# A message-passing kernel on one core: operands in PSUM, loads in turn, stores placed anew

## The chip, the cores and the metric

The kernel runs on one core of a Trainium2 chip. The metric is the device time of one execution in microseconds (us), as the median of several runs. The engines are PE (matrix products; PEld is its weight load), DVE (VectorE), ACT (ScalarE), POOL (GpSimd) and SP (SyncE, which here only issues transfers). Each works through its own queue of instructions in order, and semaphores tie them together. SBUF is the on-chip memory that all of them read; PSUM is the small memory into which PE writes its products, in banks[...].

## What is computed

A graph has 12,500 nodes with 96 features and 412,500 edges, which are sorted by their target node. Three small layers, each with a batch norm over all its rows, give node features, edge features and messages; the messages are summed per target.

```python
def _mlp(h, W, b, gamma, beta):
    h = relu(h @ W + b)
    mu, var = mean(h, axis=0), mean(square(h - mu), axis=0)
    return gamma * (h - mu) * rsqrt(var + EPS) + beta

node_feat = _mlp(x, W_node, ...)
edge_feat = _mlp(edge_attr, W_edge, ...)
row, col = edge_index
message = concatenate([x[row], x[col], edge_feat], axis=1)
message = _mlp(message, W_msg, ...)
agg = segment_sum(message, col)
out = layernorm(x + agg + node_feat)
```

## The kernel before

**Tables.** x[row] @ W_msg's first third is the same for all edges of a source node, so the kernel makes a table of it for all nodes, p_tab in DRAM, and for the targets q_tab. `table()` (L144 to L160) makes either in 7 stretches of 14 blocks: products of x (`xp`, in SBUF) with the weights (L154), copies to `trow` by DVE and ACT (L156, L158), a store (L159), then a `yield`, at which the caller puts other work in between. The loads of x in 7 chunks (L96 to L98) alternate between SP's and ACT's queues, all ahead of everything else, and the source numbers `src` follow on ACT (L99).

**Gathers.** Edges are worked on in tiles of 128, groups of 4 tiles and blocks of 4 groups: 202 blocks. A tile's 128 rows of p_tab are fetched by one indirect transfer that POOL issues (L166), 16 for a block. The first 26 blocks are gathered early, while the other stages run: `blocks()` (L171 to L178) gathers a block into one of two tiles `stage`, and SP stores it to `spill` in DRAM (L177), from where the main loop reads it back as `pb`. Each `next(store)` sets one such step in SP's and POOL's order. The first 3 blocks gather rows of x, not of p_tab, and are converted later. The other 176 blocks are gathered into a ring of 25 group tiles `pg`, the first 25 of them after the last early block (L357), each other one when an older tile has been used.

**Stages.** First p_tab, 0 to about 84 us. Then small loads (L190 to L201), and `rel` (L203 to L223), each edge's target less the first target of its block: a subtraction on DVE (L209) of `basei` from `dsti`, where `basei` is the row `base` broadcast to 128 partitions by a transfer (L207). Then q_tab, `places()` (L225 to L243), which subtracts `first` from the targets in another layout (L239) and stores them, `nodes()` (L245 to L275: the node layer, its norm, and x + node_feat sent to DRAM as `y0_d`), and `edge_norm()` (L277 to L329), which runs the edge layer over all edges for its mean and variance: products L294 into PSUM, ReLU by ACT L298, statistics by DVE L300. It loads its input and yields every 8 blocks. In these stages SP and POOL keep the order in which the program lists their work (`manual_schedule`). The places of `next(store)`: after stretches 2 and 5 of p_tab; 0, 2 and 5 of q_tab, and once after it; after steps 0, 4 and 10 of `nodes()`; and in `edge_norm()` spread over its yields by `73 * i >= 50 + 100 * n`.

**Main loop** (L502 to L534), about 1030 to 5250 us. A step k is a group; all engines keep the listed order. In step k: `linear(k+1)` (L447 to L453, PE: z from edge features and target rows, 4 tiles of 96 columns), `message(k)` (L455 to L473, DVE and ACT), `sums(k-2)` (L484, PE: sums per target in a window of 31 nodes, and the Gram matrix for the norm), once per block `edges` (L437, PE) and `prepare` (L444 ACT, L445 DVE) for the next block and `add` (L497, L498, DVE) for an older one; then POOL's gathers for a tile further ahead. In `message`, at the first group of a block (i == 0), DVE writes into h for the whole block which of 31 nodes each edge belongs to (L461: `rel` is compared with `iota`, 4 x 31 node numbers in SBUF). Then hs = z + pg (L467) for the group, which frees its ring tile, and after every second group ACT's ReLU (L469). I call the four sums of a block hs0 to hs3, and block s's first z z(4s). Per block DVE's order is L461, hs0, hs1, hs2, L445, L497 twice, L498, hs3. z has two PSUM tiles, used in turn.

After the loop a last stage (L705 on) applies the message norm and the layer norm per node.

Of the kernel before, what the change touches and what calls it, by code (L numbers as in the profile page):

```python
# [11 lines left out]
F32 = mybir.dt.float32  # L12
I32 = mybir.dt.int32
AF = mybir.ActivationFunctionType
OP = mybir.AluOpType
# [61 lines left out]
def gnn(ctx, tc, t):  # L77
# [15 lines left out]
    ring = rpool.enter_context(tc.tile_pool(name="ring", bufs=RING))  # L93
    xp = xpool.enter_context(tc.tile_pool(name="x", bufs=1)).tile([C, XW], F32, name="xp")
    nc.scalar.dma_start(w_msg, t["L0_gnn_W_msg"].rearrange("(s k) f -> k s f", k=C))
    for i in range(0, NB, CH):  # L96
        part = slice(COL[i], COL[i + CH] if i + CH < NB else XW)
        (nc.scalar if i // CH % 2 else nc.sync).dma_start(xp[:, part], t["xp"][:, part])  # L98
    nc.scalar.dma_start(src, t["src"])  # L99

    ident = const.tile([P, P], F32, name="ident")
    make_identity(nc, ident)
# [18 lines left out]
    agg = const.tile([C + 1, WT], F32, name="agg")  # L121
    rel = const.tile([P, NGP, GT], F32, name="rel")
    base = const.tile([1, NBL], I32, name="base")
    mstat = const.tile([C, 2], F32, name="mstat")
    vec = const.tile([C, len(_VECS)], F32, name="vec")
    v = {name[7:]: vec[:, i:i + 1] for i, name in enumerate(_VECS)}
# [17 lines left out]
    def table(out, w, work, ps, queues, bufs):  # L144

        rows = out.rearrange("(p b) f -> p b f", b=NB)
        for c in range(0, NB, CH):
            r = work.tile([P, CH, C], F32, name="trow", bufs=3)
            for j, i in enumerate(range(0, CH, NBK)):
                n = min(NBK, CH - i)  # L150
                pt = ps.tile([P, NBK, C], F32, name="pt", bufs=bufs)
                for g in range(n):
                    k = COL[c + i + g]
                    nc.tensor.matmul(pt[:, g, :], xp[:, k:k + P], w, start=True, stop=True)  # L154
                if j % 2:
                    nc.scalar.activation(r[:, i:i + n, :], pt[:, :n, :], AF.Copy)  # L156
                else:
                    nc.vector.tensor_copy(r[:, i:i + n, :], pt[:, :n, :])  # L158
            queues[c // CH % len(queues)].dma_start(rows[:, c:c + CH, :], r)  # L159
            yield  # L160
# [18 lines left out]


    store = blocks()
    with tc.manual_schedule(engines={ET.SP, ET.Pool}):
        with tc.tile_pool(name="win_w", bufs=1) as work, tc.tile_pool(name="win_ps", bufs=2, space=PSUM) as ps:
            for i, _ in enumerate(table(p_tab, w_msg[:, 0, :], work, ps, (nc.sync, nc.scalar), 4)):
                if i in (2, 5):
                    next(store)

# [2 lines left out]
    nc.sync.dma_start(vec, t["vecs"])  # L190
    nc.sync.dma_start(w_node, t["L0_gnn_W_node"])
    nc.sync.dma_start(b_msg, t["L0_gnn_b_msg"])
    nc.sync.dma_start(base, t["base"])
    for i in range(NS):
        k, n = Q * i, C - Q * i
        nc.sync.dma_start(wide[k:k + EK, :n], t["wb"][:, C - n:])
# [6 lines left out]
    with tc.tile_pool(name="win", bufs=1) as win, tc.tile_pool(name="win_ps", bufs=2, space=PSUM) as ps:  # L203
        dsti = win.tile([P, NGP, GT], I32, name="dsti")
        nc.sync.dma_start(dsti, t["dst"].rearrange("p (g t) -> p g t", t=GT))
        basei = win.tile([P, NBL], I32, name="basei")
        nc.sync.dma_start(basei, t["base"].to_broadcast([P, NBL]))  # L207
        by_block = "p (b g) t -> p b (g t)"
        nc.vector.tensor_tensor(rel.rearrange(by_block, g=BG), dsti.rearrange(by_block, g=BG),  # L209
                                basei.unsqueeze(2).to_broadcast([P, NBL, BG * GT]), op=OP.subtract)  # L210
        worst = win.tile([P, 2, BG], F32, name="worst")
        for k in range(BG):
            nc.vector.tensor_reduce(worst[:, 0, k:k + 1], rel[:, k:NG:BG, :], axis=AX.XY, op=OP.max)
            nc.vector.tensor_reduce(worst[:, 1, k:k + 1], rel[:, k:NG:BG, :], axis=AX.XY, op=OP.min)
        out = win.tile([P, 1], F32, name="out")
        nc.vector.tensor_sub(worst[:, 0, :], worst[:, 0, :], iota[:, :, WN - 1])
        nc.vector.tensor_sub(worst[:, 1, :], iota[:, :, 0], worst[:, 1, :])
        nc.vector.tensor_reduce(out, worst.rearrange("p a k -> p (a k)"), axis=AX.X, op=OP.max)
        po = ps.tile([1, P], F32, name="po", bufs=1)
        nc.tensor.transpose(po, out, ident)  # L220
        most = win.tile([1, 1], F32, name="most")
        nc.vector.tensor_reduce(most, po, axis=AX.X, op=OP.max)
        nc.vector.tensor_scalar(flag, most, 0.0, None, op0=OP.is_gt)  # L223

    def places():  # L225

        with tc.tile_pool(name="lin", bufs=2) as work, tc.tile_pool(name="lin1", bufs=1) as one:
            first = one.tile([P, RW], I32, name="first")
            nc.sync.dma_start(first, t["first"])
            rows = rel_d.rearrange("o (p g e) -> (o p) g e", g=RW, e=GE)  # L230
            parts = [slice(i, min(i + 2, RW)) for i in range(0, RW, 2)]
            lins = []
            for i in range(len(parts) + 1):
                if i < len(parts):
                    n = parts[i].stop - parts[i].start
                    lins.append(work.tile([P, n, GE], I32, name="lin"))
                    nc.sync.dma_start(lins[i], t["dlin"][:, parts[i], :])
                    rlin = work.tile([P, n, GE], F32, name="rlin")
                    nc.vector.tensor_tensor(rlin, lins[i], first[:, parts[i]].unsqueeze(2).to_broadcast([P, n, GE]),  # L239
                                            op=OP.subtract)  # L240
                    lins[i] = rlin
                if i:
                    nc.sync.dma_start(rows[:, parts[i - 1], :], lins[i - 1])  # L243
# [87 lines left out]
    def fast(ring):  # L331
# [3 lines left out]
        with tc.manual_schedule(engines={ET.SP, ET.Pool}):  # L335
            with tc.tile_pool(name="tab_w", bufs=1) as work, tc.tile_pool(name="tab_ps", bufs=2, space=PSUM) as ps:
                for i, _ in enumerate(table(q_tab[WM:WM + NN, :], w_msg[:, 1, :], work, ps, (nc.sync,), 8)):
                    if i in (0, 2, 5):
                        next(store)
            next(store)  # L340
            nc.sync.dma_start(q_tab[:WM, :], zero[:WM])
            for r in range(WM + NN, WT, 64):
                n = min(64, WT - r)
                nc.sync.dma_start(q_tab[r:r + n, :], zero[:n])
            places()
            for i, _ in enumerate(nodes()):
                if i in (0, 4, 10):
                    next(store)
            xpool.close()
            n = 0  # L350
            for i, _ in enumerate(edge_norm()):
                if 73 * i >= 50 + 100 * n:
                    next(store, None)
                    n += 1
            for _ in store:
                pass
            got = {g: ahead_of(g) for g in range(SPILL, SPILL + RING)}  # L357
# [11 lines left out]
        with tc.tile_pool(name="fix", bufs=1) as fix, tc.tile_pool(name="msg", bufs=2) as work, \  # L369
# [11 lines left out]
            hb = [fix.tile([P, BG, GT, P], F32, name=f"h{i}") for i in range(HB)]  # L381
            for x in hb:
                nc.vector.memset(x[:, :, :, C:C + 1], 1.0)

            eas, block, prs, zs, pas, pair = {}, {}, {}, {}, {}, [None]

# [60 lines left out]
            def linear(k):  # L447
                s, g = steps[k]
                n = min(GT, NT - g * GT)
                zs[k] = ps.tile([P, GT, C], F32, name="z")  # L450
                for i in range(n):
                    nc.tensor.matmul(zs[k][:, i, :], left[s % 2][:KR, g % BG, i * P:(i + 1) * P],  # L452
                                     rhs[:KR, s % RB, g % BG, :], start=True, stop=True)  # L453

            def message(k):  # L455
                s, g = steps[k]
                n = min(GT, NT - g * GT)
                i = g % BG
                h, z, pg = hb[s % HB], zs.pop(k), got.pop(g)
                if i == 0:  # L460
                    nc.vector.tensor_tensor(  # L461
                        h[:, :, :, C + 1:C + 1 + WN], rel[:, g:g + BG, :].unsqueeze(3).to_broadcast([P, BG, GT, WN]),
                        iota.unsqueeze(2).to_broadcast([P, BG, GT, WN]), op=OP.is_equal)
                if i % 2 == 0:
                    pair[0] = work.tile([P, 2, GT, C], F32, name="hs")
                hs = pair[0]
                nc.vector.tensor_add(hs[:, i % 2, :n, :], z[:, :n, :], pg[:, :n, :])  # L467
                if i % 2 and n == GT:
                    nc.scalar.activation(h[:, i - 1:i + 1, :, :C], hs, AF.Relu)  # L469
                elif i % 2 or g == NG - 1:  # L470
                    for o in range(i // 2 * 2, i + 1):
                        m = GT if o < i else n
                        nc.scalar.activation(h[:, o, :m, :C], hs[:, o % 2, :m, :], AF.Relu)  # L473
# [301 lines left out]
```

## Time and profile before

| what | value |
|---|---|
| median of 3 runs | 5365.1 us (5362.86 to 5375.22) |
| profiled execution | 5383.58 us; its span, first to last instruction, 5381.9 us |
| granted clock of PE, mean | 0.662 |
| 0 to 284 us: tables, rel, places, nodes | POOL busy 157.4 us, PE 156.7, DVE 118.1 |
| 284 to 980 us: edge_norm | PE busy 401.4 us, DVE 359.3, POOL 336.8, ACT 293.0 |
| 1030 to 5250 us: main loop | PE busy 2717.8 us, POOL 2594.5, PEld 2133.8, DVE 1153.4, ACT 697.9 |
| 5250 to 5382 us: last groups, last stage | PE busy 108.3 us, DVE 78.3 |

The slices of the span, each a fortieth (134.5 us):

```profile
PE   5557653566666666666666666666666666765668
DVE  1446542622222222223222223222232223222225
POOL 5553455255566666666666665666666666666660
PEclk9755555566766666666676676666666666667667
```

A digit is the busy share in tenths; the last row is the clock that PE was granted, in tenths of full speed. Slices 1 and 2 are the tables and nodes, 3 to 7 edge_norm, 8 to 39 the main loop, 40 the end. A row of a group of instructions, as the profile has it, gives line, engine, operation, output<-inputs with shapes and count, then the busy time in all and the mean of one in ns, then the idle time of the engine just before them and what ended most of it. A timeline row gives the start, the duration, the engine and line, and in brackets the idle time before it and what ended it.

### The profile page before, as it was taken

What the parts mean: (1) busy time and instruction counts of PE and PEld (TensorE: products, weight loads), DVE (VectorE), ACT (ScalarE), POOL (GpSimd) and SP (SyncE); (2) the same over time, 40 slices, a digit from 0 to 9 for tenths busy, and PEclk for the clock granted to TensorE, in tenths of its full rate; (3) what the DMA queues carried; (4) which work ended last, traced back from release to release, by engine and by line L of the source; (5) the groups of instructions that cost most, each with busy time, mean ns of one, the idle gap of its engine ahead of it and who ended that gap; (6) DMA issues with size and microseconds to landing.
All of it is one profiled execution on the core that took longest, in us unless ns stands there. A gap on an engine that the chain in (4) does not pass through costs nothing. (4 is left out here: it accounts for less than half of the span.)

```text
span 5381.9 us, 46696 instructions
## 1 busy us (share of the span) xinstructions
PE 3389.5 (63%) x16705; PEld 2576.6 (48%) x16705; DVE 1708.3 (32%) x2635; ACT 1077.3 (20%) x1015; POOL 3088.7 (57%) x3231
## 2 busy tenths in 40 slices
PE   5557653566666666666666666666666666765668
PEld 5423321354545555445554445454555544554557
DVE  1446542622222222223222223222232223222225
ACT  0235432311111111111111111111111111111112
POOL 5553455255566666666666665666666666666660
PEclk9755555566766666666676676666666666667667
DMA  5333322111111111111111111111111111111112
GB/s 165 127 87 66 71 62 50 27 37 33 39 44 37 43 43 43 44 37 43 43 43 41 45 36 43 43 42 44 37 43 42 42 45 36 43 43 42 45 36 83
DMA packets 154401, 270.78 MB, mean 50 GB/s; under 512 B 83463, under 2 KB 83976, under 8 KB 153154
## 3 DMA queue, kind: packets, MB, share of 16 engines
q0 software_dynamic: 103136, 158.62, 13.8%
q1 hardware_dynamic: 47936, 98.39, 6.4%
q10 hardware_dynamic: 3088, 10.71, 0.6%
q8 instruction: 133, 2.18, 0.2%
q14 instruction: 108, 0.88, 0.1%
HBM read 225.88 MB, written 41.60 MB: 50 GB/s over the span
## 5 line engine op out<-in xcount | busy, mean ns | idle before, releaser
L166 POOL DMA_INDIRECT pg<-p_tab,src x2807 | 2689.2, 958 | 1785.6 <-DVE hs L467 953.3
L452 PE MATMUL z<-rhs,left 128*128 128x96 f32 x6446 | 1221.4, 337 | 886.4 <-issue 766.5
L452 PEld LDWEIGHTS z<-rhs,left 128*128 128x128 f32 x6446 | 1094.8, 248 | 1181.1 <-issue 987.6
L484 PE MATMUL pa<-h 128*97 128x128 f32 x6446 | 1241.8, 331 | 522.8 <-issue 519.7
L484 PEld LDWEIGHTS pa<-h 128*97 128x97 f32 x6446 | 1012.0, 209 | 628.3 <-issue 626.2
L467 DVE TENSOR_TENSOR hs<-z,pg 128x384 f32<-128x384 f32 x702 | 384.7, 555 | 2634.4 <-remote 1730.7
L469 ACT ACTIVATE h<-hs 128x768 f32<-128x768 f32 x402 | 339.7, 845 | 2891.3 <-DVE hs L467 1768.6
L294 PE MATMUL pr<-ea,wide 10*128 10x512 f32 x1212 | 403.1, 1074 | 296.3 <-issue 197.6
L166 POOL DMA_INDIRECT stage<-p_tab,src x368 | 352.9, 959 | 355.8 <-DMA spill<-stage 224.6
L437 PE MATMUL pr<-ea,we 6*127 6x512 f32 x1404 | 458.7, 856 | 80.9 <-issue 67.9
L444 ACT ACTIVATE left<-pr 96x2048 f32<-96x2048 f32 x202 | 377.2, 1867 | 641.5 <-remote 452.0
L445 DVE TENSOR_SCALAR left<-pr 31x2048 f32<-31x2048 f32 x202 | 462.8, 2291 | 130.7 <-ACT left L444 84.2
L300 DVE BATCH_NORM_STATS2 estats<-r 128x6 f32<-128x512 f32 x606 | 365.5, 701 | 333.9 <-issue 217.8
L294 PEld LDWEIGHTS pr<-ea,wide 10*128 10x128 f32 x1212 | 203.3, 321 | 494.8 <-issue 316.3
L298 ACT ACTIVATE r<-pr 128x1024 f32<-128x1024 f32 x303 | 296.3, 1026 | 459.2 <-remote 261.4
L437 PEld LDWEIGHTS pr<-ea,we 6*127 6x127 f32 x1404 | 133.4, 235 | 255.1 <-issue 241.8
L461 DVE TENSOR_TENSOR h<-rel,iota 128x496 f32<-128x496 f32 x202 | 134.8, 667 | 0.0
L154 PE MATMUL pt<-w_msg,xp 96*128 96x96 f32 x392 | 89.3, 422 | 61.8 <-issue 38.5
L497 DVE TENSOR_TENSOR agg<-pa,agg 97x62 f32 x404 | 90.1, 223 | 105.0 <-remote 78.8
L154 PEld LDWEIGHTS pt<-w_msg,xp 96*128 96x128 f32 x392 | 85.5, 330 | 65.4 <-issue 50.6
L467 DVE TENSOR_TENSOR hs<-z,pb 128x384 f32<-128x384 f32 x104 | 57.2, 554 | 177.7 <-PE z L452 82.4
L498 DVE TENSOR_TENSOR gram<-pa,gram 97x388 f32<-97x388 f32 x202 | 111.4, 551 | 0.0
(107 smaller groups left out, 611.5 us busy)
## 6 DMA issues: line engine op xcount, KB each, us to landing
pg<-p_tab,src POOLq DMA_INDIRECT x2807
spill<-stage SPq DMA_DIRECT2D x26, 768.0 KB
pb<-spill SPq DMA_DIRECT2D x26, 768.0 KB
ea<-in_ea SPq DMA_DIRECT2D x75, 160.0 KB
rhs<-q_tab SPq DMA_DIRECT2D x202, 46.5 KB
ea<-in_ea SPq DMA_DIRECT2D x352, 20.0 KB
stage<-p_tab,src POOLq DMA_INDIRECT x368
q_tab<-trow SPq DMA_DIRECT2D x7, 672.0 KB
```

Source lines behind the costliest of these rows:

```text
L154: nc.tensor.matmul(pt[:, g, :], xp[:, k:k + P], w, start=True, stop=True)
L166: nc.gpsimd.indirect_dma_start(out=pg[:, i, :], out_offset=None, in_=tab[:, :], in_offset=bass.IndirectOffsetOnAxis(ap=idx[:, k:k + 1], ax ...
L294: nc.tensor.matmul(pr[:, k % 2, :], wide[Q * i:Q * i + 2 * EK, :], ea[Q * i:Q * i + 2 * EK, b % J, :], start=True, stop=True)
L298: nc.scalar.activation(r, pr, AF.Relu)
L300: nc.vector.bn_stats(stats[:, (k - o) % NS, (k - o) // NS, :], r[:, 1 - o, :])
L437: nc.tensor.matmul(prs[s][:C + WN, i, :], we[Q * i:Q * i + EK + 1, :], block[s][Q * i:Q * i + EK + 1, :], start=True, stop=True)
L444: nc.scalar.activation(x[:C, :n, :], pr[:C, :n, :], AF.Relu)
L445: nc.vector.tensor_scalar(x[C:C + WN, :n, :], pr[C:C + WN, :n, :], 0.0, None, op0=OP.is_equal)
L452: nc.tensor.matmul(zs[k][:, i, :], left[s % 2][:KR, g % BG, i * P:(i + 1) * P], rhs[:KR, s % RB, g % BG, :], start=True, stop=True)
L467: nc.vector.tensor_add(hs[:, i % 2, :n, :], z[:, :n, :], pg[:, :n, :])
L469: nc.scalar.activation(h[:, i - 1:i + 1, :, :C], hs, AF.Relu)
L484: nc.tensor.matmul(pas[s][:, g % BG, :C + 1 + WN], h[:r, i, :C + 1], h[:r, i, :C + 1 + WN], start=i == 0, stop=i == n - 1)
```

## The change

It has four parts.

1. In the main loop z gets two fixed PSUM tiles of a whole bank, `zb[0]` and `zb[1]`, used in turn as before. Columns 384 to 507 of `zb[0]`, which z does not use, hold a copy of `iota`, `nodes_of`, written once. The comparison (L461) reads `nodes_of` in place of `iota`.
2. `rel`: the broadcast by a transfer is replaced by a product of a column of ones with `base` as f32, into PSUM, from where the subtraction reads it. `places`: `first` is copied to PSUM as f32, and the subtraction reads it there.
3. Only the first 4 chunks of x are loaded ahead; chunk i + 4 is loaded after stretch i of p_tab, in turn on SP and ACT, and `src` after stretch 3. `base` is loaded on SP at the beginning. ACT keeps its listed order in this stage.
4. A store is set before `nodes()`, those in `nodes()` come after steps 0, 3, 7 and 11, and the formula of `edge_norm()` is unchanged, so that 11 instead of 9 stores lie before `edge_norm()` and its last comes at yield 20 instead of 23.

```diff
+    def load_x(i):
         part = slice(COL[i], COL[i + CH] if i + CH < NB else XW)
         (nc.scalar if i // CH % 2 else nc.sync).dma_start(xp[:, part], t["xp"][:, part])
-    nc.scalar.dma_start(src, t["src"])
+
+    for i in range(0, 4 * CH, CH):
+        load_x(i)
...
     base = const.tile([1, NBL], I32, name="base")
+    nc.sync.dma_start(base, t["base"])
...
-    with tc.manual_schedule(engines={ET.SP, ET.Pool}):
+    with tc.manual_schedule(engines={ET.SP, ET.Pool, ET.Activation}):
...
             for i, _ in enumerate(table(p_tab, w_msg[:, 0, :], work, ps, (nc.sync, nc.scalar), 4)):
+                if (i + 4) * CH < NB:
+                    load_x((i + 4) * CH)
+                if i == 3:
+                    nc.scalar.dma_start(src, t["src"])
                 if i in (2, 5):
                     next(store)
...
-        basei = win.tile([P, NBL], I32, name="basei")
-        nc.sync.dma_start(basei, t["base"].to_broadcast([P, NBL]))
+        ones = win.tile([1, P], F32, name="ones")
+        nc.vector.memset(ones, 1.0)
+        basef = win.tile([1, NBL], F32, name="basef")
+        nc.vector.tensor_copy(basef, base)
+        pb = ps.tile([P, NBL], F32, name="pb", bufs=1)
+        nc.tensor.matmul(pb, ones, basef, start=True, stop=True)
...
-                                basei.unsqueeze(2).to_broadcast([P, NBL, BG * GT]), op=OP.subtract)
+                                pb.unsqueeze(2).to_broadcast([P, NBL, BG * GT]), op=OP.subtract)
...
-            first = one.tile([P, RW], I32, name="first")
-            nc.sync.dma_start(first, t["first"])
+            firsti = one.tile([P, RW], I32, name="firsti")
+            nc.sync.dma_start(firsti, t["first"])
+            first = ps.tile([P, RW], F32, name="first")
+            nc.vector.tensor_copy(first, firsti)
...
             places()
+            next(store)
             for i, _ in enumerate(nodes()):
-                if i in (0, 4, 10):
+                if i in (0, 3, 7, 11):
                     next(store)
...
+            zb = [ps.tile([P, GE], F32, name=f"z{i}", bufs=1) for i in range(2)]
+            nodes_of = zb[0][:, GT * C:GT * C + BG * WN].rearrange("p (k w) -> p k w", w=WN)
+            nc.vector.tensor_copy(nodes_of, iota)
...
-                zs[k] = ps.tile([P, GT, C], F32, name="z")
+                zs[k] = zb[k % 2][:, :GT * C].rearrange("p (t c) -> p t c", c=C)
...
-                        iota.unsqueeze(2).to_broadcast([P, BG, GT, WN]), op=OP.is_equal)
+                        nodes_of.unsqueeze(2).to_broadcast([P, BG, GT, WN]), op=OP.is_equal)
```

More of the change, by code (lines that the diff above doesn't have):

```diff
@@ L95, in gnn @@
     nc.scalar.dma_start(w_msg, t["L0_gnn_W_msg"].rearrange("(s k) f -> k s f", k=C))
-    for i in range(0, NB, CH):
+    def load_x(i):
         part = slice(COL[i], COL[i + CH] if i + CH < NB else XW)
         (nc.scalar if i // CH % 2 else nc.sync).dma_start(xp[:, part], t["xp"][:, part])
-    nc.scalar.dma_start(src, t["src"])
+    for i in range(0, 4 * CH, CH):
+        load_x(i)
     ident = const.tile([P, P], F32, name="ident")
@@ L192, in gnn @@
     nc.sync.dma_start(b_msg, t["L0_gnn_b_msg"])
-    nc.sync.dma_start(base, t["base"])
     for i in range(NS):
@@ L225, in places @@
     def places():
-        with tc.tile_pool(name="lin", bufs=2) as work, tc.tile_pool(name="lin1", bufs=1) as one:
-            first = one.tile([P, RW], I32, name="first")
-            nc.sync.dma_start(first, t["first"])
+        with tc.tile_pool(name="lin", bufs=2) as work, tc.tile_pool(name="lin1", bufs=1) as one, \
+                tc.tile_pool(name="lin_ps", bufs=1, space=PSUM) as ps:
+            firsti = one.tile([P, RW], I32, name="firsti")
+            nc.sync.dma_start(firsti, t["first"])
+            first = ps.tile([P, RW], F32, name="first")
+            nc.vector.tensor_copy(first, firsti)
             rows = rel_d.rearrange("o (p g e) -> (o p) g e", g=RW, e=GE)
```

## The prediction

> **What bounds the kernel now.** I read first the forty slices and the costliest groups, then the busy time by stage, then the main loop's waits and single rows.
>
> ```profile
> PE 3389.5 (63%) x16705; PEld 2576.6 (48%) x16705; DVE 1708.3 (32%) x2635; ACT 1077.3 (20%) x1015; POOL 3088.7 (57%) x3231
> L166 POOL DMA_INDIRECT pg<-p_tab,src x2807 | 2689.2, 958 | 1785.6 <-DVE hs L467 953.3
> L461 DVE TENSOR_TENSOR h<-rel,iota 128x496 f32<-128x496 f32 x202 | 134.8, 667 | 0.0
> ```
>
> No engine is full. POOL's 2807 gathers are busy 2689.2 us and wait 1785.6 us; 953.3 of that is for hs (L467), which frees ring tiles. (Its longest, 132.5 us, is the step from the early stages to the main loop.) L461 never waits, 0.0. The windows view tells more: matmuls and gathers are not independent.
>
> ```profile
> 780.00:800.00 20.00, 4.16 (x8) 1.01 (x8) 2.58 (x4) 2.05 (x2) 15.12 (x17) 0.50 0.19 40
> 920.00:940.00 20.00, 20.00 (x71) 11.87 (x72) 20.00 (x35) 17.54 (x19) 0.00 (x0) 0.50 0.40 81
> 5200.00:5300.00 100.00, 81.92 (x521) 65.40 (x521) 42.18 (x65) 26.47 (x23) 33.30 (x35) 0.80 0.13 32
> ```
>
> Columns: stretch, its length, PE, PEld, DVE, ACT, POOL (busy, count), clock, DMA share, GB/s. In edge_norm PE does 8 matmuls in 20 us while POOL gathers without a break, and 71 when POOL is silent, at the same clock 0.50. In the main loop PE does 317 per 100 us (3000 to 3100) and 521 where gathering ends. So gathers starve PE, PE's late z keeps hs late, hs keeps the ring full, POOL pauses, PE recovers. From 1033 to 5250 us POOL has 2707 gathers: 2594.6 us busy, 770.3 in gaps of 0.3 us, and 185 pauses that sum to 852.2. Shorter gathers or shorter pauses shorten the run; a longer hs after a pause lengthens it.
>
> **is_equal from PSUM: the gain.** A gather takes 0.947 us. This view shows an exception:
>
> ```profile
> 3012.47 1.50 POOL L166 DMA_INDIRECT pg<-p_tab,src  x1 [0.31 <-DMA pg<-p_tab,src]
> 3012.48 0.67 DVE L461 TENSOR_TENSOR h<-rel,iota 128x496 f32<-128x496 f32 x1
> ```
>
> The gather that meets L461 lasts 1.50 us. Over the trace gathers that overlap L467, L445, L498 or L300 average 945 to 947 ns; those with L461 and L467 1160 (133 of them), with L461 alone 1119 (34). Over 947 ns the main loop loses 34.5 us. The Trainium skill's "SBUF — State Buffer", section "Who interferes with whom", says why: a VectorE instruction with two SBUF inputs contends with GpSimd's SBUF reads, and one side blocks whole. L461 reads rel and iota; hs has one input in PSUM. With iota in PSUM the rule gives back all 34.5. L461 keeps its 667 ns: of two sums over 768 elements in the last stage, L729 with one input in PSUM takes 947 ns, L737 with both in SBUF 954. Not all 34.5 arrive: where a pause's end is set by PE's recovery alone, POOL only starts to wait sooner. I take 27, ends 0 and 34.5.
>
> **The cost: a new wait.** The copy lies in columns 384 to 507 of zb[0], the bank into which z(4s) is written. The changed program's order shows L461 waiting for the last matmul of z(4s), hs0 behind it. The skill's "PSUM — Partial Sum Buffer", section "PSUM bank collisions raise a hardware error", speaks against the change here: guard by bank, not by address, so the wait isn't an accident of the build. What that is worth stands in the rows:
>
> ```profile
> 2476.85 0.56 DVE L467 TENSOR_TENSOR hs<-z,pg 128x384 f32<-128x384 f32 x1 [2.55 <-remote]
> 2477.32 0.67 DVE L461 TENSOR_TENSOR h<-rel,iota 128x496 f32<-128x496 f32 x1
> 2489.89 1.02 DVE L467 TENSOR_TENSOR hs<-z,pg 128x384 f32<-128x384 f32 x2 [11.91 <-remote]
> ...
> 2490.72 0.95 POOL L166 DMA_INDIRECT pg<-p_tab,src  x1 [4.16 <-DVE hs L467]
> ```
>
> Today L461 runs in the shade of DVE's 11.91 us wait for z. Then hs0 starts at 2489.89, and POOL, paused 4.16 us, goes on 0.83 later. Changed, L461 starts when hs0 did; hs0, hs1 (same row), ACT's relu and POOL's next gather come 0.667 us later. Behind L461 on DVE stand all of the block's sums, L445 and L497; PE waits for z's buffer and for h. hs0 begins at least 0.667 after L461's end in 84 of 202 blocks; counted block by block the delay sums to 109 us. What counts is the 79 pauses that hs0 ends: 43 us in all, 34.8 in pauses under 4.6 us and 8.5 in those of 8 to 9. Ends: 0 and +43. A paused POOL is also when PE runs free, so some of the longer pause comes back as matmuls done before the next stall: I take half, +21. By the first rule alone the loop would be 34.5 faster; by rows of both parts, −27 + 21 = **−6** (−34 to +43).
>
> PE's other changes: one semaphore instruction per block, already satisfied (202 beside 14,160 matmuls), and fixed tiles for two rotating ones, the same reuse after the same hs. Nothing.
>
> **rel and places.** The 128-row broadcast of base (L207) goes: one of SP's DMAs, 908 to 907. In come a memset, a copy of 202 values, one matmul. L209's idle time of 11.5 us is ended by that broadcast, but dst, issued just before, lands at nearly the same time, so the path gains −1, bounds −2 to +2. L209 and L239 held POOL 2.4 and 1.9 us; the early gathers wait for stores, so these reach nothing. places gets a small copy before its subtract, under 1 us beside its loads.
>
> **x and src in turn.** SP's queue has this before any stretch of p-table is stored:
>
> ```profile
> 30.56 0.26 SPq L196 DMA_DIRECT2D wide<-in_wb  x1
> 31.57 0.26 SPq L197 DMA_DIRECT2D wide<-in_wb  x1
> 31.93 0.37 SPq L159 DMA_DIRECT2D p_tab<-trow  x1
> ```
>
> The first trow is complete near 16 us (ACT's copy at 15.31 for 0.33), its store goes out at 31.93, behind vec, w_node and wide, which wait for the transfers of x. With four x loads up front this comes some 14 us earlier; three more x loads, then src, follow the stores on SP and ACT in order. The three trow buffers come free earlier. But PE also crawls there, from 36 to 72 us, under gathers of x, and a late x chunk is now possible. Bounds −14 and +10; I take −5. Block 3's gathers (88.1) wait for this table.
>
> **Stores.** A store on SP frees one of two stage tiles and lets POOL make 16 gathers, 19.7 us. Before: 2 in p-table, 3 in q-table, one before places, 3 in nodes, the rest in edge_norm. After: S6 comes before nodes, four in nodes, so 11 lie before edge_norm instead of 9; the last of them goes at its yield 20 instead of 23. SP's loads of ea and stores of y0 are passed, under 3 us of issue each. Price in edge_norm: from 430.9 to 746.9 us there are 13 yields and 10 stores; a yield takes 13.65 us where POOL is silent (937 to 964), so (316 − 13 × 13.65)/10 = 13.9 us a store. Two go: −28. They are paid in nodes, where POOL is busy 47 of 90 us and the DVE, ACT, PE chain has slack between: ends 4 and 14 each; I take 8 to 9, +17. The 100 ring gathers after the last store (775.6 to 900.4) starve PE as before. Net −11, bounds −20 to +5.
>
> **Sum.** −6 −1 −5 −11 = −23. The profiled execution takes 5383.6 us (span 5381.9 and 1.7 around it), 18.5 above the median of 5365.1; changed it would take 5360.6, the median 5342: 0.43% less. A measurement here can tell 0.3%, 16 us, from no change.
>
> **Rivals.**
> - *Contention goes, pauses stay.* If L461's wait falls where PE is the bound anyway: −34.5 in the loop, −20 early, **5310**. For: the long pauses are PE's. Against: hs0 ends more pauses than any other sum (79 of 185). Chance 0.22.
> - *Paid back.* If each end of a gather stretch is set by PE's recovery, faster gathers just meet a later hs: loop 0, early −5, **5360**, no change. For: pauses with the same 16 or 20 gathers between them (133 of 184). Against: a pause starts PE's recovery, and it starts earlier. Chance 0.24.
> - *The new wait decides.* Place: L461 between z(4s) and hs0. Price 0.667 us per delayed pause and no matmuls won back: 79 pauses cost 53 against 17 where half the gain is lost, early −5: **5396**. Were all 109 us passed on, through sums and edges, to pauses that hs1 to hs3 end, 109 − 27 − 8 would give 5439. It decides from 34.5/0.667 = 52 pauses lengthened by the full price. For: 84 blocks qualify. Against: only 43 of the 109 us stand on a pause. Chance 0.24.
> - *It doesn't do what it says* (gathers still long): the wait without the gain, inside the last range; 0.03.
>
> **Numbers.** My forecast has 0.27. Its own range is 5325 to 5352; with the rivals 5298 to 5402, since the farthest ends (all early gains on top of all of the loop's; 109 us) hold less than 2 in 10. Faster: forecast nearly whole, 0.25, the first rival's 0.22, and 0.03 of the second's: 0.50. Same: 0.21 of the second and 0.02 of the forecast: 0.23. Slower: 0.27.
>
> **What would show it.** Gathers that overlap is_equal average 947 ns, POOL's mean row drops from 958 to 947; is_equal gets idle time ended by z (it had 0.0), and hs0 loses as much. The loop's pauses rise from 852 to some 873 us. edge_norm's first to last yield shortens by about 28 us and nodes grows by about 17; p-table's first store goes out near 17 us. Wrong: pauses up by more than 35 us, nodes longer by 28, or gathers that stay long.

## The result: slower by 0.67%

Measured beside each other, before took 5368.7 us in the median (5362.9 to 5375.2, 4 runs) and the changed kernel 5402.5 us (5398.1 to 5405.2, 4 runs): a ratio of 1.0067, interval 1.005 to 1.0085. That is 34 us more, where 23 fewer were forecast. The profiled execution of the changed kernel took 5399.9 us, that of before 5383.6, 15 above its median, so the two traces differ by 16 us only, and what they miss has to be found by timed runs. By the traces the loss is made early: the first gather into a ring tile that has been used comes at 1061.5 us instead of 1032.9, 28.6 later, while from it to the last gather the loop takes 4203 us instead of 4217.

The costliest groups of the changed kernel, to be set beside those of before:

```profile
L170 POOL DMA_INDIRECT pg<-p_tab,src x2807 | 2655.0, 946 | 1832.1 <-DVE hs L487 1014.1
L481 DVE TENSOR_TENSOR h<-rel,z 128x496 f32<-128x496 f32 x202 | 135.2, 669 | 605.8 <-remote 271.0
```

Both halves of the loop's part are there as foreseen. A gather takes 946 ns in the mean, not 958, and POOL is busy 34 us less in this row; is_equal keeps its length (669 ns) and waits 605.8 us, where it waited 0.0. What POOL waits for hs rises from 953.3 to 1014.1 us. The loop's pauses sum to 871 us where they summed to 852; 873 had been forecast.

The windows view, now by stage: nodes with what is left of places, then edge_norm. First before, then changed (length, then PE, PEld, DVE, ACT, POOL, clock, DMA share, GB/s):

```profile
194.00:290.00 96.00, 47.74 (x207) 43.83 (x206) 53.33 (x61) 19.53 (x19) 50.43 (x54) 0.54 0.37 113
290.00:982.00 692.00, 402.94 (x1212) 203.10 (x1212) 360.05 (x598) 294.69 (x302) 333.74 (x353) 0.50 0.29 62
```

```profile
194.00:343.00 149.00, 74.28 (x243) 51.07 (x241) 54.98 (x61) 30.67 (x36) 70.37 (x75) 0.57 0.27 86
343.00:1010.00 667.00, 402.31 (x1212) 207.05 (x1212) 359.82 (x598) 295.45 (x302) 309.32 (x328) 0.50 0.28 60
```

edge_norm is 25 us shorter, near the 28 forecast, and POOL does 25 gathers fewer beside it. But nodes is 53 us longer, not 17. Nearly all of that lies in its first part, the node products pn. This is the view of that line (duration minimum, median, maximum; first and last start; then what ended the idle time of PE and of its weight loads, PEld, the two added up), before and changed:

```profile
L252 PE MATMUL pn<-xp,w_node x50: 342/592/1166, 174.6 to 197.3; 96*96 96x512 f32 x48, 96*96 96x212 f32 x2
```

```profile
L266 PE MATMUL pn<-xp,w_node x50: 342/851/1169, 190.9 to 245.7; 96*96 96x512 f32 x48, 96*96 96x212 f32 x2
...
  ACT agg L267: 54.2, 16
  issue: 51.7, 33
```

They start 16 us later and take 55 us, not 23. The windows view of that stretch, first before, then changed:

```profile
174.00:184.00 10.00, 9.58 (x19) 3.63 (x19) 0.00 (x0) 5.58 (x9) 7.55 (x8) 1.00 0.81 288
184.00:194.00 10.00, 10.00 (x24) 3.75 (x23) 4.33 (x4) 6.98 (x11) 8.00 (x7) 1.00 0.78 263
194.00:204.00 10.00, 3.61 (x10) 1.30 (x8) 7.83 (x14) 4.11 (x6) 7.56 (x9) 0.91 0.28 75
```

```profile
191.00:201.00 10.00, 10.00 (x16) 3.60 (x17) 4.14 (x6) 4.10 (x6) 7.56 (x9) 1.00 0.51 170
201.00:211.00 10.00, 5.11 (x9) 1.13 (x7) 1.38 (x2) 1.37 (x2) 7.56 (x9) 0.84 0.16 39
211.00:221.00 10.00, 4.04 (x4) 0.79 (x4) 1.38 (x2) 1.37 (x2) 7.56 (x9) 0.50 0.16 39
221.00:231.00 10.00, 3.34 (x4) 0.79 (x4) 1.38 (x2) 1.37 (x2) 7.49 (x8) 0.50 0.16 39
231.00:241.00 10.00, 6.42 (x8) 2.00 (x8) 3.85 (x6) 4.02 (x7) 0.00 (x0) 0.50 0.02 5
```

Changed, PE has 16 records in the first 10 us, then 9, 4 and 4, while POOL gathers without a break (busy 7.56 of each 10 us); when POOL stops at 231 it recovers within a few us. These are the few products beside gathers of the prediction's first rows, met at a place where the prediction did not look. They do not begin with the gathers: before, POOL gathers without a break from 174 to 216 us, and PE gets through all its products at full pace, by 197.6. Changed, POOL gathers from 171 to 231, 48 in a row instead of 32, since the store ahead of nodes goes out at 192.9 (the next one before went at 228.4), and the products start 20 us into it.

In the slow stretch they come in this rhythm:

```profile
212.16 0.68 ACT L267 ACTIVATE agg<-pn,vec 96x512 f32<-96x512 f32 x1 [4.23 <-remote]
212.89 2.02 PE L266 MATMUL pn<-xp,w_node 96*96 96x512 f32 x2 [2.89 <-ACT agg L267]
```

PE waits for ACT to empty one of the four tiles pn, and ACT waits 4 to 5 us for something that the view does not name ("remote"). "Starved" therefore stands here for few products in a stretch of gathers. Where between a product and its reading the time goes, no run shows.

### The profile page after: what moved, and what is told of

Same layout as the page of the kernel before. It is cut to its first block, busy times and chain, and to the rows that moved or that the text cites. A ratio compares the mean times of both kernels' runs of the same rounds, so it can differ in the third digit from the quotient of the medians.

```text
span 5398.2 us, 46877 instructions
## 1 busy us (share of the span) xinstructions
PE 3345.5 (62%) x16707; PEld 2588.4 (48%) x16707; DVE 1709.9 (32%) x2639; ACT 1074.0 (20%) x1015; POOL 3049.8 (56%) x3231
## 5 line engine op out<-in xcount | busy, mean ns | idle before, releaser
L170 POOL DMA_INDIRECT pg<-p_tab,src x2807 | 2655.0, 946 | 1832.1 <-DVE hs L487 1014.1
L472 PE MATMUL z<-rhs,left 128*128 128x96 f32 x6446 | 1266.9, 337 | 1027.4 <-issue 662.0
L472 PEld LDWEIGHTS z<-rhs,left 128*128 128x128 f32 x6446 | 1114.8, 248 | 1344.5 <-issue 891.2
L504 PE MATMUL pa<-h 128*97 128x128 f32 x6446 | 1224.2, 333 | 442.9 <-issue 440.3
L489 ACT ACTIVATE h<-hs 128x768 f32<-128x768 f32 x402 | 338.9, 843 | 2708.9 <-DVE hs L487 1561.5
L457 PE MATMUL pr<-ea,we 6*127 6x512 f32 x1404 | 389.6, 779 | 78.2 <-issue 65.4
L481 DVE TENSOR_TENSOR h<-rel,z 128x496 f32<-128x496 f32 x202 | 135.2, 669 | 605.8 <-remote 271.0
L457 PEld LDWEIGHTS pr<-ea,we 6*127 6x127 f32 x1404 | 111.5, 216 | 209.0 <-issue 189.7
```

What stands on the lines that cost most here:

```text
L170: nc.gpsimd.indirect_dma_start(out=pg[:, i, :], out_offset=None, in_=tab[:, :], in_offset=bass.IndirectOffsetOnAxis(ap=idx[:, k:k + 1], ax ...
L457: nc.tensor.matmul(prs[s][:C + WN, i, :], we[Q * i:Q * i + EK + 1, :], block[s][Q * i:Q * i + EK + 1, :], start=True, stop=True)
L504: nc.tensor.matmul(pas[s][:, g % BG, :C + 1 + WN], h[:r, i, :C + 1], h[:r, i, :C + 1 + WN], start=i == 0, stop=i == n - 1)
```

## The experiments

Each run was timed beside before, and before differs: it took 5360 to 5422 us beside e1 to e4, e9 to e12 and e13 to e16 (I call these runs starved), but 4166 to 4167 us beside e5 to e8 and e17, e18 (I call these free). There POOL never pauses in the loop. The stretch from 1500 to 4000 us, in e5 (kernel before, free) and in e13 (starved; its loop is that of before), and 200 us of edge_norm in e5 and in the first trace of before, in the windows view:

```profile
1500.00:4000.00 2500.00, 1556.67 (x10202) 1368.95 (x10202) 841.33 (x1277) 490.95 (x424) 1896.73 (x1979) 0.76 0.22 51
```

```profile
1500.00:4000.00 2500.00, 1626.32 (x8372) 1260.78 (x8376) 687.41 (x1048) 411.43 (x350) 1547.49 (x1624) 0.68 0.19 42
```

```profile
300.00:500.00 200.00, 200.00 (x680) 132.02 (x675) 200.00 (x339) 171.20 (x169) 149.97 (x159) 0.50 0.56 113
400.00:600.00 200.00, 131.48 (x408) 72.57 (x411) 122.11 (x204) 101.49 (x105) 82.43 (x88) 0.50 0.31 65
```

In the loop there are 1979 gathers against 1624 in the same time. In edge_norm PE has 680 products beside 159 gathers against 408 beside 88, at the same granted clock of 0.50, so there the clock is not what makes the difference. What does, no run shows. It need not be the chip: e9 to e12 and e17, e18 carry the same chip number, 0, and fell on different sides. Ratios are always to before as timed beside the run. Loop figures are from one profiled execution each; executions of one kernel scatter by up to 49 us (e14, 5382 to 5431).

### e1 and e4: the loop's part alone, in two forms

e1 adds to before only the fixed banks and the copy in PSUM. e4 puts the copy in the other bank and lists is_equal ahead of the next z, so that it waits for no product; the next z, which is written into that bank, then waits for it:

```diff
-            nodes_of = zb[0][:, GT * C:GT * C + BG * WN]...
+            nodes_of = zb[1][:, GT * C:GT * C + BG * WN]...
...
+                    if k < n and g % BG == 0:
+                        which(s, g)        # is_equal, taken out of message(k)
                     if k + 1 < n:
                         linear(k + 1)
```

> The kernel before with the main loop's part alone: z in two fixed banks, is_equal reads the node numbers from PSUM; early stages as before. Theory A (what the two traces show, 4217 us from the first to the last gather of the loop before and 4203 changed, is the change's doing): about 14 us faster than before, ratio 0.9974. Theory B (the profiled execution of before was 15 us above its median, and its loop was long by chance): gain and new wait cancel, ratio 0.999 to 1.001. Theory C (the new wait outweighs the gain): over 1.002. In all of them gathers average 946 ns.

> The kernel before with the main loop's part in another form: the node numbers lie beside z in the other bank, zb[1], and is_equal is listed ahead of the next z, so that it reads a bank whose z has been used and waits for no product; gathers lose their contention all the same. If the new wait of is_equal is what took back the gain: 25 to 35 us faster than before, ratio 0.993 to 0.995, is_equal's idle time near 0, pauses about as long as before (852 us). If faster gathers only meet later sums whatever is_equal does: as the run with the loop's part alone.

Measured: e1 1.0028 (1.0017 to 1.0039), e4 1.0027 (1.0019 to 1.0036). Theory C for e1, and for e4 the second case, the same as e1. Gathers were at 946 ns or below in both. So the loop's part is slower by some 15 us, although it takes some 34 us of work off POOL; theory A had rested on the two first traces, in which the changed loop is 14 us shorter. But e4 does not settle the reason, since in it PE waits for is_equal; from the view of its z line, what ended the idle time of PE and PEld (of the 446.4 us, 206.9 are PE's own):

```profile
  issue: 961.2, 749
  DVE h L460: 446.4, 109
  DVE left L449: 440.4, 158
```

### e6 and e10: the fixed banks alone

```diff
-                zs[k] = ps.tile([P, GT, C], F32, name="z")
+                zs[k] = zb[k % 2][:, :GT * C].rearrange("p (t c) -> p t c", c=C)
```

> The kernel before with z in two fixed banks alone; is_equal reads iota from SBUF and waits for nothing, as before. PE's stream has the same additional waits on its own work as in the changed kernel. Theory A (the additional waits on PE, one semaphore instruction a block, cost what the two runs of the loop's part lost): 10 to 20 us slower, ratio 1.002 to 1.004. Theory B (the fixed banks cost nothing): 0.999 to 1.001.

> The fixed banks alone again, wanted on a chip on which gathers starve PE. If one more semaphore instruction a block on PE costs there what e1 and e4 lost: ratio 1.002 to 1.004. If not: 0.999 to 1.001. On a chip without pauses: 1.0005 as in e6.

Measured: 1.0005 (0.9997 to 1.0014) where PE isn't starved, 0.9998 (0.9988 to 1.0009) where it is. The banks and the additional semaphore instructions on PE (511 in e10's trace from 1000 us on, 311 before) cost nothing, as forecast.

### e7 and e9: the contention alone

```diff
-                    nc.vector.tensor_tensor(
+                    nc.vector.tensor_scalar(
                         h[:, :, :, C + 1:C + 1 + WN], rel[:, g:g + BG, :]...,
-                        iota.unsqueeze(2).to_broadcast([P, BG, GT, WN]), op=OP.is_equal)
+                        0.0, None, op0=OP.is_equal)
```

The kernel then leaves out the window sums; it serves for the time alone.

> The kernel before with is_equal replaced by a comparison of rel with a constant, so that one SBUF input is left, with no other bank, wait or semaphore changed; the window sums are left out by it. Gathers should fall to 946 ns. Theory A (time that gathers gain shortens the loop): 25 to 35 us faster, ratio 0.993 to 0.995. Theory B (PE, starved while gathers run, needs its time without them, and a gather that is held is such time; the pauses grow by what the gathers gain): 0.998 to 1.002, pauses some 35 us longer than before.

> The comparison of rel with a constant again (the window sums left out), wanted on a chip on which gathers starve PE (before at 5360 to 5430 us), since on the chip of e7 POOL never paused in the loop. Theory A (time that gathers gain shortens the loop there too): ratio 0.993 to 0.996. Theory B (pauses grow by what the gathers gain, since PE needs a given time free of gathers): 0.998 to 1.002. Theory C (a held gather lets PE run, so that without contention PE starves more): over 1.002. On a chip without pauses: 0.9934 as in e7.

Free (e7): 0.9934 (0.992 to 0.9948), 27 us: theory A. Starved (e9): 0.9982 (0.9973 to 0.9992), 9 us: near theory B. This instruction is also shorter (416 ns for 667), so the 9 us are, if anything, too many for the contention. In e9's trace the loop's gathers are busy 2558.8 us where fixed banks alone (e10, timed in the same set) have 2579.7, and the pauses sum to 857.3 where those have 835.5: the 21 us that gathers gained by these two traces went back into pauses. The rows of e10 and e9:

```profile
L166 POOL DMA_INDIRECT pg<-p_tab,src x2807 | 2674.0, 953 | 1765.1 <-DVE hs L469 928.8
L166 POOL DMA_INDIRECT pg<-p_tab,src x2807 | 2653.2, 945 | 1786.6 <-DVE hs L467 953.4
L461 DVE TENSOR_SCALAR h<-rel 128x496 f32<-128x496 f32 x202 | 84.1, 416 | 0.0
```

In e9 gathers take 945 ns instead of 953, and POOL's wait for hs is 953.4 us instead of 928.8.

### e8 and e11: the wait alone

With fixed banks, is_equal still on two SBUF inputs:

```diff
                 if i == 0:
+                    nc.vector.tensor_copy(late, zb[0][:1, :1])
                     nc.vector.tensor_tensor(
```

> The kernel before with fixed banks and, ahead of is_equal, a copy of one element of z's first bank, so that is_equal waits for z(4s) as in the changed kernel but still reads two SBUF inputs. Theory A (the wait costs 0.667 us for each delayed pause, nothing won back): 40 to 50 us slower, ratio 1.008 to 1.010. Theory B (pauses come from PE's recovery and take up the wait): within 0.2% of the run with fixed banks alone. Contention may shrink, where is_equal now runs while POOL pauses.

> The wait of is_equal for z(4s) again, without the second input in PSUM, wanted on a chip on which gathers starve PE. Theory A (0.667 us in each delayed pause, nothing won back): ratio 1.006 to 1.010. Theory B (PE's recovery takes the wait up): 0.999 to 1.002. On a chip without pauses: 0.997 as in e8, where the wait moved is_equal away from some gathers.

e11: 1.0045 (1.0031 to 1.006), 24 us, between the two theories and close to the prediction's 21. The pauses sum to 865.3 us, 30 above e10's. With e9's 9 us against it the sum is +15 us: what e1 lost. It is not the wait quite alone: the added copy takes 0.146 us itself, which adds to the cost, and gathers that overlap is_equal lose 15 us over 947 ns where in e10 they lose 25, which takes from it. Nor do the pauses that hs0 ends grow, which the prediction counted: they fall from 88 (472 us) in e10 to 62 (435 us), and those that hs1 and hs2 end rise from 84 (292 us) to 97 (362 us). e8, where PE isn't starved: 0.997 (0.9958 to 0.9982), faster than either theory had it. There the wait costs nothing, and it moved is_equal away from some gathers: their excess over 947 ns fell from 38.5 us (e5) to 23.8.

> The kernel before, unchanged, to have its trace on the same chip as the runs beside it, since chips differ by up to 1%. Every theory expects ratio 1.000; the loop's gathers sum some 34 us more busy time than in the runs with the comparison's second input in PSUM, and if the gain was taken back, some 35 to 50 us less in pauses.

e5 took 4170 us, as before beside it, and is the trace of before used above for the free runs.

### e12: everything but the loop's part

> The kernel before with all of the change but the main loop's part: rel, places, loads of x and src in turn, stores. On a chip on which gathers starve PE, theory A (node products wait for first's PSUM tile and then run under gathers, and nodes loses more than edge_norm wins): 15 to 29 us slower, ratio 1.003 to 1.005, with the node products from 191 to about 246 us. If the loop's part is to blame for most of the 34 us: 0.999 to 1.001. On a chip without pauses nothing is starved, and the products' later start of 16 us is all: 1.000 to 1.004.

Measured: 1.0058 (1.0044 to 1.0072), 27 to 31 us: theory A, a little beyond its 1.005. So the early stages carry most of the loss. The view of the node products' line in e12:

```profile
L266 PE MATMUL pn<-xp,w_node x50: 342/592/1169, 189.7 to 244.9; 96*96 96x512 f32 x48, 96*96 96x212 f32 x2
...
  ACT agg L267: 58.5, 17
  issue: 29.7, 32
  DVE rlin L253: 19.1, 1
```

The last line is the wait that the prediction missed: PE stands 19.1 us until rlin of places (L253) has read first for the last time. Places' PSUM tile holds space that pn's buffers take, so nodes can no longer begin beside places.

### e2, e3, e13, e14, e15: which half of the early part

Undone one by one: first back in SBUF (e2 with the loop's part, e13 without), the stores at their old places (e3, e14), both (e15).

```diff
-            firsti = one.tile([P, RW], I32, name="firsti")
-            nc.sync.dma_start(firsti, t["first"])
-            first = ps.tile([P, RW], F32, name="first")
-            nc.vector.tensor_copy(first, firsti)
+            first = one.tile([P, RW], I32, name="first")
+            nc.sync.dma_start(first, t["first"])
```

```diff
             places()
-            next(store)
             for i, _ in enumerate(nodes()):
-                if i in (0, 3, 7, 11):
+                if i in (0, 4, 10):
                     next(store)
```

> The changed kernel, with first in SBUF in places as before. Theory A (first's PSUM tile lies where the node products go, so these wait for the end of places and then run under gathers, starved): node products start near 171 us instead of 190.9 and end before 200 instead of 246; 35 to 45 us less than the changed kernel, ratio to before 0.998 to 1.000. Theory B (the store set ahead of nodes is to blame, since it lets POOL gather on through the node products): they start early but still end after 225, and under 16 us are won, ratio about 1.004.

> The changed kernel, with the stores placed as before. Theory A (first's PSUM tile): node products still start near 191 us, run until POOL's gathers pause near 211 and end near 225; some 20 us won there, 13 more in the y0 part of nodes, and 25 to 28 lost in edge_norm, so -5 to -10 against the changed kernel, ratio 1.005. Theory B (the stores): the node products end near 200, -25 us against the changed kernel, ratio 1.002.

> All of the change but the loop's part, with first in SBUF as before (stores at their new places). On a chip on which gathers starve PE: node products start near 172 us, but POOL gathers on until 230 and they end near 220, as in e2; edge_norm begins some 33 us later and is some 21 shorter: 12 us slower, ratio 1.001 to 1.0035. If first's PSUM tile alone is to blame for the loss: 0.999 or less.

> All of the change but the loop's part, with the stores placed as before (first in PSUM). On a chip on which gathers starve PE: node products from 190 to about 228 us as in e3, edge_norm some 7 us later and as long as before: 5 us slower, ratio 1.000 to 1.002. If first's PSUM tile alone is to blame: 1.005.

> Loads of x and src in turn and rel's product alone: first in SBUF, stores and loop as before. q_tab was complete some 3 us sooner in the changed kernel. Expected 2 to 5 us faster, ratio 0.999 to 1.000. If the loads in turn hurt: over 1.001.

| run | first | stores | loop | ratio (interval) |
|---|---|---|---|---|
| e12 | PSUM | new | before | 1.0058 (1.0044 to 1.0072) |
| e13 | SBUF | new | before | 1.0032 (1.0021 to 1.0043) |
| e14 | PSUM | old | before | 1.0019 (1.0008 to 1.0029) |
| e15 | SBUF | old | before | 0.9997 (0.9982 to 1.0011) |
| e2 | SBUF | new | changed | 1.0054 (1.004 to 1.0067) |
| e3 | PSUM | old | changed | 1.0048 (1.0034 to 1.0063) |
| e1 | SBUF | old | changed | 1.0028 (1.0017 to 1.0039) |

Neither suspect is alone. Against e15 the stores' new places cost 0.0035, some 19 us, first in PSUM 0.0022, some 12 us; together 0.0057, against e12's 0.0058 in another set. From the runs' intervals I estimate each difference to be uncertain by 0.002, some 10 us, so the share of first is only just clear of noise. The traces agree: the loop's first gather into a used ring tile comes at 1041.7 us in e15, at 1062.7 in e13 and at 1058.4 in e14. e2 and e3 say the same over e1: 0.0026 and 0.0020. The loads in turn, with rel's product, are worth nothing that can be measured. Taken singly, e2 came near its theory B (the stores) and e3 near its theory A (first); the table shows that both are at work. The node products' lines of e13, e14 and e15 show the two ways:

```profile
L263 PE MATMUL pn<-xp,w_node x50: 561/592/1169, 174.8 to 233.4; 96*96 96x512 f32 x48, 96*96 96x212 f32 x2
```

```profile
L266 PE MATMUL pn<-xp,w_node x50: 342/592/1168, 196.1 to 232.7; 96*96 96x512 f32 x48, 96*96 96x212 f32 x2
```

```profile
L263 PE MATMUL pn<-xp,w_node x50: 561/592/1169, 171.6 to 214.2; 96*96 96x512 f32 x48, 96*96 96x212 f32 x2
```

e13's begin early but last to 233: the store ahead of nodes frees a stage tile at once, and POOL, which in e15 falls silent from 212 to 241, gathers on to 235. e14's begin late and end at the same time. e15's end near 214. These must be compared within one set: with the early stages of before the products end at 197 to 200 us in the first trace and in e9 to e11, at 213 in e16, and at 224 and 229 in e1 and e4.

### e16, e17, e18: is there a better place for is_equal?

e16 lists is_equal of the next block ahead of that block's first z, so that on DVE it stands between gram and hs3. e17 keeps both inputs in SBUF and only makes z(4s+1) wait for is_equal, by a copy of one element of zb[1] behind it. e18 is e4 again.

```diff
+                        which(k + 1)       # e16: is_equal, if k + 1 begins a block
                         linear(k + 1)
```

> The kernel before with the node numbers in zb[0], and is_equal for the next block listed just ahead of that block's first z: on DVE it then stands between gram and hs3, reads a bank whose z has been used, and what waits for it is z(4s), which waits for left in any case. Theory A (in e4 the next z's wait for is_equal cost what the gathers gained): on a chip on which gathers starve PE 0.997 to 0.9985, like e9. Theory B (moving the numbers to PSUM costs something of its own): 1.002 to 1.004 as e4. On a chip without pauses: 0.992 to 0.994.

> The kernel before with fixed banks, is_equal on two SBUF inputs at its place, followed on DVE by a copy of one element of zb[1], so that the next z, z(4s+1), waits for is_equal as in e4. On a chip on which gathers starve PE, theory A (that wait costs what is_equal's own wait cost in e11, and e4 is the sum of it and of what e9 won): ratio 1.003 to 1.006. Theory B (PE's wait is free, and the numbers in PSUM cost something in themselves): 0.999 to 1.001. On a chip without pauses: near 1.000.

> e4 again, beside e17. Theory A: e17's ratio less about 0.002, near 1.002 to 1.004. Theory B: 1.002 to 1.004 too, with e17 at 1.000. On a chip without pauses: 0.992 to 0.995.

e16: 1.0099 (1.0079 to 1.0119), the slowest of all, and starved. Both theories missed it. hs3 now comes behind L449, two L505, gram and is_equal, pauses rise to 942 us, and those that hs3 ends to 68 (155 us), where e15 in that set has 35 (112 us). That is 43 of some 75 us of additional pauses. It fits the reading that 0.667 us in DVE's busy stretch is dearer than in the shade of hs0's wait, where before has it; but z(4s), and by the trace ACT's ReLU 24 times, wait for is_equal in e16 as well, and no run takes these apart.

e17 and e18 turned out free: 0.9996 (0.9987 to 1.0004), as forecast for that, and 0.9914 (0.99 to 0.9927), a little faster than the 0.992 forecast. e18's rows:

```profile
L166 POOL DMA_INDIRECT pg<-p_tab,src x2807 | 2648.5, 944 | 856.6 <-issue 786.0
L460 DVE TENSOR_TENSOR h<-rel,z 128x496 f32<-128x496 f32 x202 | 133.4, 661 | 0.0
```

Here POOL's gathers are the bound (e17 has 2683.4 us in that row), and all of their 35 us arrive. So that kernel beats before by 0.86% in a free set and loses 0.27% in a starved one (e4). What PE's wait for is_equal costs where PE is starved, and so whether it explains e4, stays open. No version that computes the whole was found to beat before in the starved sets. The changed kernel itself wasn't run in a free one.

## Why the prediction was wrong

- **What bounds the kernel**: right. Gathers starve PE, and the pauses are its recovery. The prediction used this for the loop and for edge_norm, and not for nodes.
- **"places gets a small copy before its subtract, under 1 us beside its loads."** This step failed. The copy is that small; but its target, a PSUM tile, holds the space of pn's buffers until places ends, and PE waited 19.1 us (e12). With the starvation behind it the cost was some 12 us (e14 against e15), where the prediction had nothing.
- **"They are paid in nodes ... ends 4 and 14 each; I take 8 to 9, +17."** This one failed more. The two stores won in edge_norm most of what was forecast (28; the traces show 25 in the whole change, 21 for e13 against e15), but nodes paid 42 us for them (edge_norm's first product at 338.9 in e13, at 296.7 in e15), not 17. The stores' part alone came out at +19 net (e13 against e15) instead of −11. The y0 part paid about 14 for its additional store (57 to 71 us long), the upper end of the forecast; what was missed is that a store just ahead of the node products turns 32 gathers in a row into 48, at the one place of nodes where PE has a row of 50 matmul records to do. "Slack between" was read from sums over the stage.
- **x, src and rel**: −5 and −1 forecast, nothing measured (e15). q_tab's last store goes out 3 us sooner in the changed kernel, and p-table's first at 16.1 as forecast, but neither reaches the end.
- **"I take 27, ends 0 and 34.5."** The contention went wholly (946 ns), as the Trainium skill's "SBUF — State Buffer", section "Who interferes with whom", lets expect of an operand outside SBUF, and won 9 us (e9) where PE is starved, not 27. The second rival's argument, that faster gathers only meet a later hs, was most of the truth. Where PE isn't starved, all of it arrives (e18).
- **"I take half, +21."** The size was right: 24 (e11). That is in part luck: the pauses that hs0 ends, on which it was counted, became fewer (79 before, 52 changed), and those that hs1 and hs2 end more (80 and 118). Sum of the loop: +15 (e1), not −6.

With the measured terms, 19 + 12 − 2 for the early part and 24 − 9 for the loop give 44 us, 0.8%, within the interval of 1.0067 (0.5 to 0.85%), though they come from several sets of runs, and 10 us above the measured 34. The rival that ended slower named 5396 us and the right wait in the loop, but had the early stages as a gain; that its total came near is luck.

## What to carry to other kernels

Shortening an engine's instructions pays only where that engine's own work sets the pace; where another one is held up by it and must recover, the time comes back as longer pauses. A PSUM tile in a stage that used none can end that stage's overlap with the next, so ask whose buffers lie there. And when work is moved from a costly stage to a cheaper one, look at what stands at the very place it goes to, not at the stage's average.

## What the runs showed that was not expected

The same program took 5360 to 5422 us in some sets of runs and 4166 us in others, with PE starved beside gathers in the first and not in the second; the sign of a change followed it (e4 1.0027, e18 0.9914; e11 1.0045, e8 0.997). The mean granted clock differs as well over a run, 0.66 to 0.67 against 0.74 to 0.75, though in edge_norm it is 0.50 in both. An operand in PSUM neither lengthened nor shortened is_equal (669 ns against 667).
